# A fourth of twelve products for GpSimd in the second stage, with B brought by transfers

## The chip, the cores and the metric

The kernel runs on one core of one Trainium2 chip. The metric is the device time of one execution in microseconds (us), the median of several runs. All data are float32. A core has five engines with a queue of their own each: TensorE (PE in the profile, its weight loads PEld), VectorE (DVE), ScalarE (ACT), GpSimd (POOL), and SyncE (SP), which here issues nearly all transfers.

## The reference

Three stages follow one another on a batch of four images of 192 channels and 64 x 64 pixels: two Mamba layers read forwards (first stage), one Mamba layer with a depthwise convolution and an MLP (second stage), and a window network (third stage). The change is in the second stage's Mamba layer. Cut to what matters, with `L` = 4096 positions, 384 channels `d` and 16 states `n`:

```python
xz = xf @ in_w.T;  xm, z = split(xz)
xm = silu(conv1d(xm) + conv_b)                 # 3 taps
dt, B, C = split(xm @ x_w.T)                   # 12 + 16 + 16 rows
delta = softplus(dt @ dt_w.T + dt_b)
for t in range(L):                             # per channel d and state n
    h[d, n] = exp(delta[t, d] * A[d, n]) * h[d, n] + delta[t, d] * xm[t, d] * B[t, n]
    y[t, d] = sum_n h[d, n] * C[t, n]
y = (y + xm * D) * silu(z)
out = y @ out_w.T
```

## The kernel before

**Tiles.** Positions are cut into tiles of `T` = 512, so the second stage has 4 x 8 = 32 units (image, tile). The 384 x 16 states of a unit lie in 12 blocks; a block k is a tile of 128 partitions (16 channels x 8 states) by four column groups j of 512 positions. `unit["order"]` says in which order a unit takes its blocks; q counts the places 0 to 11 in it. Blocks 2p and 2p+1 form pair p: they have the same channels and differ in the half of the states, so they share the operands of their pair (`dtE`, delta repeated for the states; `dtxE`, delta times xm repeated), while `B` and `C` belong to one of the two halves of the states ("parity" k % 2).

**A step.** `Scans.run` goes through 32 x 48 steps, step i being column group j = i % 4 of the block at place q. `Scans.step` issues for it:

- `decay` (L923) for step i + 2: ScalarE makes dA = exp(dtE * A) in one of three PSUM buffers;
- `step` (L929): VectorE's scan of 512 positions over dA and h;
- at j = 3, `read` (L945): GpSimd multiplies the block's h by C, 128 x 2048; `keep` (L940) saves the states; `sum` (L955) lets TensorE add the states of a channel with four small matmuls, some steps later; and after every fourth block `skip` (L979, VectorE) and `gate` (L985, GpSimd) finish 128 channels;
- `product` (L916): h = dtxE * B for a whole block, 128 x 2048. For the places in `shared`, which are (3, 7, 11) here, GpSimd makes it, into `h_apart`, out of `Bs`, a copy of B that a transfer has spread over the partitions (`bring_B`). For the other nine VectorE makes it at the end of the block before, into `h`, out of `B`, which TensorE spreads with one matmul into a PSUM bank (`spread`, L886) out of `dbl`. In this stage h_apart has 1 buffer, h has 3.

**Transfers.** `load` (L879) brings the `dtE` of a pair at an even place and the `dtxE` at an odd one, each with four transfers of 256 KB (16 rows, repeated 8 times), two to three places ahead; both have 2 buffers. Their sources r_dt and r_dtx are DRAM rows, written by `front` once per unit. SyncE's queue takes all of them in program order, and a transfer that has to wait holds back those behind it.

**Work beside the scans.** Everything else of the stage (layer norms, projections, taps, the next unit's `front`, the output projection `back`, the convolution and the MLP) is cut into pieces. `Behind.tick` issues pieces after every step from five lanes, as far as a budget of TensorE and ScalarE time allows. The evictions of PSUM banks are put off by some steps (`later`), and the tables `AHEAD` (keys `l_...` for the evictions, `w_...` for waits between pieces) and the `wait=` numbers of the pieces set by how many. An activation with a table of its own (Silu, Softplus, Gelu) is a `burst`: it may go only where the next block's product is VectorE's (`edge`), and costs a table load before and after it. The order on each engine is thus fixed when the program is built.

**Fronts.** During unit n, `front` of unit n + 1 runs: projection, taps, Silu, `dbl`, the three `dt` evictions (L781), Softplus (L788), delta times xm on GpSimd (L789), the two stores to r_dt and r_dtx (L794), then the three z projections (L745, evicted at L754) and their Silu (L806).

Of the kernel before, what the change touches and what calls it, by code (L numbers as in the profile page):

```python
# [30 lines left out]
KX = 68  # L31
# [219 lines left out]
class Timeline:  # L251
# [131 lines left out]
AHEAD = {  # L383
    "a_back0": 0,
    "a_cv00": 2,
# [10 lines left out]
    "b_z": 2,  # L396
    "l_dt": -1,
    "l_dw": 1,
    "l_hid": 1,
    "l_mean1": 2,  # L400
    "l_o": 0,
    "l_out": 1,
    "l_rb2": 0,
    "l_tap": 0,
    "l_var1": 2,
    "l_var2": 0,
    "l_x": 1,
    "l_z": -1,
    "w_h1": 0,
    "w_h2": 4,  # L410
    "w_h3": 1,
    "w_in1": 0,
    "w_sq1": 2,
}

# [258 lines left out]
class Mamba:  # L674
# [3 lines left out]
    def __init__(  # L678
# [8 lines left out]
        self.nc, self.name, self.taps, self.ex, self.scan = nc, name, taps, ex, scan  # L687
        self.order = (1, 0, 2, 3, 4, 5, 7, 6, 9, 8, 10, 11) if summed else range(NQ)
        self.z_b = None
# [43 lines left out]
    def front(self, xn, first, u):  # L733
# [31 lines left out]
        for d in range(ND):  # L765
            nc.tensor.matmul(ps, self.x_w[:, d, :], xc[:, d, :], start=(d == 0), stop=(d == ND - 1))
        dbl = u["dbl"] = self.work.tile([KX, T], F32, name="dbl", bufs=2 if self.summed else 1)
        h = behind.later(lambda ps=ps: nc.scalar.copy(dbl, ps), name="x")
        halves = []
        for d in range(ND):  # L770
            yield Piece(0.85, bank=True, after=[h], wait=(1 if d else 3) if self.summed else (0 if d else 2))
            if d == 0:
                bc = u["bc"] = self.dram.tile([2 * NS, T], F32, name="r_bc", bufs=3)
                nc.sync.dma_start(bc, dbl[RK : RK + 2 * NS, :])
                dt = self.work.tile([128, ND, T + 4], F32, name="dt", bufs=1)[:, :, 3 : 3 + T]
                dtx = raw[:, :, K - 1 :]
            ps = behind.bank([128, T], "ps_dt")
            nc.tensor.matmul(ps, self.dt_w[:, bass.ts(d, 128)], dbl, start=True, stop=True)
            halves.append(
                behind.later(  # L780
                    lambda d=d, ps=ps: nc.scalar.activation(  # L781
                        dt[:, d, :], ps, AF.Identity, bias=self.dt_b[:, d : d + 1]
                    ),
                    name="dt",
                )
            )
# [10 lines left out]
        u["rows"] = rows  # L797
        z = u["z"] = self.work.tile([128, ND, T + 4], F32, name="z", bufs=2)[:, :, 1 : 1 + T]
        made = []
        for d in range(ND):  # L800
            if d:
                yield Piece(1.7, bank=True, wait=0)
            made.append(project(ND + d, z[:, d, :]))

        def silu():
            nc.scalar.activation(z, z, AF.Silu)  # L806
            u["silu"] = True
            yield Piece()
# [37 lines left out]
    def sum_taps(self, raw, projected, u):  # L846
# [3 lines left out]
        for d in range(ND):  # L850
# [6 lines left out]
            for j, o in enumerate((raw[:, d, 2:], one[:, d, 1:], xc[:, d, :])):  # L857

                def tap(o=o, ps=ps, d=d, j=j):
                    nc.scalar.activation(  # L860
                        o, ps, AF.Identity, scale=self.conv_w[:, d, j : j + 1], bias=self.tap_b[:, d, j : j + 1]
                    )

                h = behind.later(tap, bank=(j == 2), more=j, name="tap")
            halves.append(h)
        yield Piece(after=halves, wait=2)
        nc.gpsimd.tensor_copy(self.halo[:, :, :2], raw[:, :, T:])
# [6 lines left out]
    def load(self, u, pair, i):  # L874

        t = u["rows", pair, i] = self.work.tile([128, 4, T], F32, name=("dtE", "dtxE")[i], bufs=2)
        for j in range(4):
            row = 128 * (pair // 2) + 32 * j + 16 * (pair % 2)
            self.nc.sync.dma_start(  # L879
                t[:, j, :], u["rows"][i][row : row + 16, :].unsqueeze(1).broadcast_to([16, 8, T])  # L880
            )

    def spread(self, u, o, last):

        B = u["B", o] = self.psum_a.tile([128, T], F32, name="B" if self.summed else f"B{o}", bufs=1)
        self.nc.tensor.matmul(B, self.ex.spread[:, o, :], u["dbl"], start=True, stop=True)  # L886
        u["spread"][0] = last
# [14 lines left out]

    def bring_B(self, u, o):
        v = self.work.tile([128, 1 + T], F32, name="Bs", bufs=1)[:, 1:]
        rows = u["bc"][8 * o : 8 * o + 8, :]
        self.nc.sync.dma_start(v, rows.unsqueeze(0).broadcast_to([16, 8, T]))
        u["Bs", o] = v

    def product(self, u, k):
        apart = k in u["apart"]  # L910
        if apart:
            h = self.work.tile([128, 4, T + 4], F32, name="h_apart", bufs=1 if self.summed else 3)
        else:
# [7 lines left out]
    def decay(self, u, k, j):  # L921
        dA = u["dA", k, j] = self.psum_a.tile([128, T], F32, name="dA", bufs=3)
        self.nc.scalar.activation(  # L923
            dA, u["rows", k // 2, 0][:, j, :], AF.Exp, scale=self.A[:, k, j : j + 1]
        )
# [48 lines left out]
    def skip(self, u, c):  # L974
        y = u["xc"][:, c, :]
        if not self.summed:
            self.nc.vector.tensor_tensor(y, u["ys"], u["z"][:, c, :], ALU.mult)
            return
        self.nc.vector.scalar_tensor_tensor(y, y, self.D[:, c : c + 1], u["ys"], ALU.mult, ALU.add)  # L979

    def gate(self, u, c):
        if not self.summed:
            return
        y = u["xc"][:, c, :]
        self.nc.gpsimd.tensor_tensor(y, y, u["z"][:, c, :], ALU.mult)  # L985


class Scans:
# [6 lines left out]
    def __init__(self, nc, units, behind):  # L995
        self.nc, self.units, self.behind = nc, units, behind
        self.due = {}
        for n, unit in enumerate(units):
            unit[1]["y_read"], unit[1]["gated"] = [False], [False]
            xcs = unit[0].xcs  # L1000
            unit[1]["xc_free"] = [units[n - xcs][1]["y_read"]] if n >= xcs else []
            unit[1]["z_free"] = [units[n - 2][1]["gated"]] if n > 1 else []
            unit[1]["spread"] = [False]
            odd = int(n % 2 and unit[0].summed)
            unit[1]["order"] = [k ^ odd for k in unit[0].order]
            unit[1]["apart"] = [unit[1]["order"][q] for q in unit[0].shared]
            dbls = 2 if unit[0].summed else 1
            unit[1]["dbl_free"] = [units[n - dbls][1]["spread"]] if n >= dbls else []

# [8 lines left out]
    def run(self):  # L1018
# [3 lines left out]
        for o in range(2):  # L1022
            if o == (u["order"][0] % 2 if m.summed else 1):
                m.spread(u, o, not m.summed)
            self.behind.add(0, m.spread_C(u, o), Piece())
        if m.summed:
            m.bring_B(u, u["apart"][0] % 2)
        for i in range(2):
            m.load(u, 0, i)
        m.load(u, 1, 1)  # L1030
        self.behind.force(lambda: m.summed or ("Bs", 0) in u)
        m.product(u, u["order"][0])
        for i in range(self.AHEAD):
            m.decay(u, u["order"][0], i)
# [12 lines left out]
    def step(self, i, n):  # L1047
# [8 lines left out]
        if j == 0 and to < n:  # L1056
            m2, u2, k2, _ = self.tile(to)
            self.behind.force(lambda: "rows" in u2)
            m2.load(u2, k2 // 2, q % 2)
        if i + self.AHEAD < n:  # L1060
# [3 lines left out]
        if m.summed:  # L1064
            if j == 0 and k not in u["apart"]:
                self.spread(i, n, m, u, k)
        elif j == 0 and q == NQ - 1 and i + 8 < n:
# [3 lines left out]
        if j == 2 and i + 6 < n:  # L1071
            m2, u2, k2, _ = self.tile(i + 6)
            if k2 in u2["apart"]:
# [5 lines left out]
                if m2.summed and i3 < n:  # L1079
                    _, u3, k3, _ = self.tile(i3)  # L1080
                    self.at(i + 6, lambda: m2.bring_B(u3, k3 % 2))
        if j == 3:
# [6 lines left out]
            if i + 1 < n:  # L1089
                m2, u2, k2, _ = self.tile(i + 1)  # L1090
                if k2 not in u2["apart"]:
                    m2.product(u2, k2)
            added, skipped, gated = (4, 6, 8) if m.summed else (8, 12, 12)
            if q % 4 == 0 and not m.summed or q + 2 in m.shared and m.summed:
                added += 1 if m.summed else 2
            self.at(i + added, lambda: self.sum(m, u, q))
            if q % 4 == 3:
                c = q // 4
                self.at(i + skipped, lambda: self.skip(m, u, c))
                self.at(i + gated, lambda: m.gate(u, c))  # L1100
                if c == ND - 1:
                    self.at(i + gated, lambda: self.gated(u, after))

    def gated(self, u, after):
# [6 lines left out]

    def spread(self, i, n, m, u, k):
        i += 4
        while i < n and i // 4 % NQ in m.shared:
            i += 4
        if i >= n:
            return
        m2, u2, k2, _ = self.tile(i)
        if u2 is u and k2 % 2 == k % 2:
            return  # L1120
        rest = [k3 for k3 in u2["order"][i // 4 % NQ :] if k3 not in u2["apart"]]
        m2.spread(u2, k2 % 2, all(k3 % 2 == k2 % 2 for k3 in rest))
        self.behind.budget -= 0.85

# [202 lines left out]
def mamba_block(tc, x, p96, p96_ap, p128, p128_ap, m_in, ex_aps, out, sums, following):  # L1327
# [4 lines left out]
    with ExitStack() as ctx:  # L1332
# [18 lines left out]
        behind.order = (4, 1, 2, 3, 0)  # L1351
        behind.bl = 0.2
        ln = NormT(nc, const, work, behind)
        ex = Expand(nc, fixed, *ex_aps)
        mamba = Mamba(
            nc, "m", 3, m_in, const, work, fixed, scan, psum_y, psum_a, dram, ln.ident, ex, behind, (3, 7, 11), True
        )
# [95 lines left out]
        def tail(b, t):  # L1453
# [33 lines left out]
            for k in range(2):  # L1487
# [3 lines left out]
                )  # L1491
            yield Piece(1.7, bank=True, wait=5, after=[taken[0]])
            xn = work.tile([CP, 2, T], F32, name="xn2", tag="xn2", bufs=1)
            yield from ln.run(x2, xn, 2)
            units[b * NT + t]["past"][0] = True
            taken[0] = [False]
            behind.add(3, end(b, t, x2, xn, taken[0]), Piece(1.7, bank=True, wait=6))

# [33 lines left out]
        def after(n):  # L1532
# [4 lines left out]
            for t2 in ([t - 1] if t else []) + ([t] if t == NT - 1 else []):  # L1537
                ended = [units[b * NT + t2 - 2]["ended"]] if b * NT + t2 > 1 else []
                behind.add(2, tail(b, t2), Piece(2.6, bank=True, after=first + ended, wait=8))

# [847 lines left out]
```

## Time and profile before

| | |
|---|---|
| median of 3 runs | 9311.5 us (9307.59 to 9312.82) |
| the profiled execution's own time | 9300.5 us |
| its span, first to last instruction | 9298.7 us |
| first scan of the second stage to the end of its last | 4836.2 to 7638 us |
| one unit of the second stage, between 5550 and 6943 us | 87.1 us |
| TensorE's granted clock in that stretch | 0.99 |
| instructions of the whole program: DVE, POOL, ACT, PE | 7419, 3104, 10008, 30312 |
| blocks whose product VectorE, GpSimd makes (whole program) | 672, 480 |

How to read it: the page lists groups of instructions by line, engine, operation and operands (out<-in), with their count, busy time and mean duration, and then the idle time of the engine just ahead of them with what ended it. "DVE L916 h<-dtxE,B" is VectorE's product and "POOL L916 h_apart<-dtxE,Bs" is GpSimd's. The view by stretches gives the busy time of each engine in a window; the view of waits says which engine waited at which line for which; the timeline lists instructions with their starts. One float32 matmul of the program shows as two MATMUL records. The profiled execution lies 11.0 us under the median.

### The profile page before, as it was taken

The numbers are of one execution on the slowest core, as the hardware profiler recorded it, in microseconds if no ns is written. First come the engines' busy times: TensorE is split into PE (matmuls) and PEld (weight loads), VectorE is DVE, ScalarE is ACT, GpSimd is POOL, SyncE is SP. The second block draws the span as 40 slices with busy tenths as digits, with TensorE's granted clock in tenths as the row PEclk, the third lists the DMA queues.
The fourth block names the chain that finished last, engine by engine and source line by source line (L and its number), as shares of the span: only waits on it lengthen the run. The fifth ranks groups of instructions, "written<-read, shape, count | busy, mean of one in ns | idle before, by whom it ended". The sixth has DMA issues, their size and how long they took to land. (4 is left out here: it accounts for less than half of the span.)

```text
span 9298.7 us, 96768 instructions
## 1 busy us (share of the span) xinstructions
PE 7726.7 (83%) x30312; PEld 3365.2 (36%) x30312; DVE 8341.9 (90%) x7419; ACT 6520.0 (70%) x10008; POOL 7213.3 (78%) x3104
## 2 busy tenths in 40 slices
PE   5777777777777777777757999999999996899998
PEld 2322323223232232322222333333333333666766
DVE  7999999999999999999959999999999985766742
ACT  5777777777777777777746777878878863454543
POOL 6999999999999999999958888888888871111100
PEclk8888888888888888888867999999999998999999
DMA  7888888888888888888846676676676653223210
GB/s 191 213 210 209 217 213 214 210 209 216 214 213 211 209 214 214 214 212 209 215 126 182 174 193 189 184 193 189 183 194 188 184 151 79 51 64 77 52 42 22
DMA packets 1025037, 1614.02 MB, mean 174 GB/s; under 512 B 251476, under 2 KB 284584, under 8 KB 1024008
## 3 DMA queue, kind: packets, MB, share of 16 engines
q1 hardware_dynamic: 1023520, 1604.52, 66.1%
q8 instruction: 239, 3.92, 0.2%
q10 hardware_dynamic: 1000, 3.30, 0.1%
q14 instruction: 278, 2.28, 0.1%
HBM read 1388.05 MB, written 219.41 MB: 173 GB/s over the span
## 5 line engine op out<-in xcount | busy, mean ns | idle before, releaser
L923 ACT ACTIVATE dA<-dtE,m_A 128x512 f32<-128x512 f32 x4608 | 3125.6, 687 | 1355.7 <-DVE h L929 1048.2
L929 DVE TENSOR_TENSOR_SCAN h<-dA,m_state,h 128x512 f32<-128x512 f32 x2688 | 3254.6, 1266 | 91.7 <-ACT dA L923 56.0
L945 POOL TENSOR_TENSOR h<-h,C 128x2048 f32<-128x2048 f32 x672 | 2565.2, 3817 | 337.7 <-DVE h L929 246.1
L929 DVE TENSOR_TENSOR_SCAN h_apart<-dA,m_state,h_apart 128x512 f32<-128x512 f32 x1920 | 2301.1, 1260 | 49.2 <-POOL h_apart L916 47.0
L916 POOL TENSOR_TENSOR h_apart<-dtxE,Bs 128x2048 f32<-128x2048 f32 x480 | 1834.9, 3823 | 78.3 <-DMA Bs<-r_bc 32.8
L945 POOL TENSOR_TENSOR h_apart<-h_apart,C 128x2048 f32<-128x2048 f32 x480 | 1833.3, 3819 | 32.9 <-DVE h_apart L929 31.5
L916 DVE TENSOR_TENSOR h<-dtxE,B 128x2048 f32<-128x2048 f32 x672 | 1519.8, 2262 | 47.5 <-DMA dtxE<-r_dtx 47.2
L955 PE MATMUL y<-h_apart,gather 128*32 128x512 f32 x3840 | 651.0, 756 | 664.2 <-POOL h_apart L945 393.9
L1781 POOL TENSOR_TENSOR d<-d,rs 128x512 f32<-128x512 f32 x64 | 85.0, 1328 | 1250.2 <-DVE rs L1776 1250.2
L745 PE MATMUL ps_in<-xT,m_in_w 96*128 96x512 f32 x1536 | 875.2, 722 | 27.7 <-ACT z L755 27.7
L955 PE MATMUL y<-h,gather 128*32 128x512 f32 x5376 | 812.3, 679 | 70.1 <-POOL h L945 66.5
L832 PE MATMUL ps_conv<-raw,m_conv 128*128 128x512 f32 x1536 | 694.5, 601 | 54.2 <-ACT raw L755 35.8
L745 PEld LDWEIGHTS ps_in<-xT,m_in_w 96*128 96x128 f32 x1536 | 341.5, 235 | 653.5 <-issue 435.5
L1465 PE MATMUL ps_dw<-strip,dw 96*96 96x512 f32 x1152 | 529.1, 605 | 0.0
L886 PE MATMUL B<-dbl,spread 68*128 68x512 f32 x384 | 263.3, 773 | 303.2 <-DVE h L916 283.6
L955 PEld LDWEIGHTS y<-h_apart,gather 128*32 128x32 f32 x3840 | 86.0, 118 | 1054.6 <-POOL h_apart L945 547.5
L832 PEld LDWEIGHTS ps_conv<-raw,m_conv 128*128 128x128 f32 x1536 | 282.3, 190 | 464.9 <-issue 417.6
L923 ACT ACT_TABLE_LOAD x343 | 440.1, 1283 | 13.6 <-DMA dtE<-r_dt 7.6
L1991 PE MATMUL unit<-xn,sed 64*128 64x256 f32 (+3 forms) x2944 | 405.5, 383 | 8.8 <-DVE d L1753 5.1
L630 PE MATMUL ps_h<-xn,t 96*128 96x512 f32 x768 | 368.3, 619 | 29.7 <-ACT xc L860 22.1
L650 PE MATMUL ps_o<-hid,t 128*96 128x512 f32 x768 | 362.9, 611 | 33.5 <-ACT hid L643 33.5
L745 PE MATMUL ps_in<-xn,m_in_w 96*128 96x512 f32 x768 | 362.5, 623 | 28.3 <-DVE xn L604 28.2
(208 smaller groups left out, 11238.3 us busy)
## 6 DMA issues: line engine op xcount, KB each, us to landing
dtE<-r_dt SPq DMA_DIRECT2D x2304, 256.0 KB, 5.8
dtxE<-r_dtx SPq DMA_DIRECT2D x2304, 256.0 KB, 4.3
r_dt<-dt SPq DMA_DIRECT2D x96, 768.0 KB, 4.6
r_dtx<-raw SPq DMA_DIRECT2D x96, 768.0 KB, 6.3
C<-r_bc SPq DMA_DIRECT2D x192, 256.0 KB, 4.9
Bs<-r_bc SPq DMA_DIRECT2D x160, 256.0 KB, 5.4
x<-x SPq DMA_DIRECT2D x64, 384.0 KB, 3.7
img<-x SPq DMA_DIRECT2D x28, 512.0 KB, 7.7
```

The source lines that it names most:

```text
L630: nc.tensor.matmul(ps, self.w1[:, k, bass.ts(m, 128)], x[:, k, :], start=(k == 0), stop=(k == 1))
L650: nc.tensor.matmul(ps, self.w2[:, m, bass.ts(k, CP)], h[:, m, :], start=(m == 0), stop=(m == NH - 1),)
L745: nc.tensor.matmul(ps, self.in_w[:, k, bass.ts(e, 128)], xn[:, k, :], start=(k == 0), stop=(k == 1))
L832: nc.tensor.matmul(ps, self.conv[:, d, j, :], raw[:, d, j : j + T], start=(j == 0), stop=(j == K - 1))
L886: self.nc.tensor.matmul(B, self.ex.spread[:, o, :], u["dbl"], start=True, stop=True)
L916: engine.tensor_tensor(h[:, :, 1 : 1 + T], u["rows", k // 2, 1], u[B, k % 2].unsqueeze(1).broadcast_to([128, 4, T]), ALU.mult)
L923: self.nc.scalar.activation(dA, u["rows", k // 2, 0][:, j, :], AF.Exp, scale=self.A[:, k, j : j + 1])
L929: self.nc.vector.tensor_tensor_scan(h[:, j, 1 : 1 + T], u.pop(("dA", k, j)), h[:, j, 1 : 1 + T], self.state[:, k, j : j + 1], ALU.mult, AL ...
L945: nc.gpsimd.tensor_tensor(h[:, :, :T], h[:, :, 1 : 1 + T], u["C", k % 2].unsqueeze(1).broadcast_to([128, 4, T]), ALU.mult)
L955: self.nc.tensor.matmul(u["ys"][32 * j : 32 * j + 32, :], self.ex.gather[:, i // 2, :], h[:, j, :T], start=(i == 0), stop=(i == 3 and self ...
L1465: nc.tensor.matmul(ps, dw[:, k, j, :], s[:, k, dy : dy + rows, dx : dx + HW], start=(j == 0), stop=(j == 8),)
L1991: nc.tensor.matmul(out, sed[p, int(h is not None), i ^ position(k, s), cols], xn[b, g].t[p, c, :], start=start, stop=stop,)
```

## The change

GpSimd makes the products at places 3, 7, 9 and 11, into two buffers of h_apart. TensorE spreads no B in this stage; for the other eight products a transfer brings B into a new tile `Bd`, and ScalarE copies it to the PSUM bank `B` where the half of the states changes, four times a unit (`fill` sets the places). `dtE` becomes a ring of five single parts (one column group each), whose four transfers are issued at four successive steps; `z` becomes a ring of five single parts, so Silu on z is three activations, and the third z projection waits until the unit before has gated its first 128 channels (`z_gate`). `dbl` has one buffer. `Bs` is brought for the next GpSimd block 2 steps after the product ahead of it is issued, where it was 6, and not where the half stays the same. `sum` is issued one step earlier. The delays of this stage (`l_...`, `w_...`, `wait=`, `bl`) have other values. The first stage's instructions are the same.

```diff
-    "l_dt": -1,
+    "l_dt": 0,
...
-    "l_o": 0,
+    "l_mean2": 1,
+    "l_o": 2,
...
+    "w_rb1": 4,
+    "w_rb2": 8,
...
-        z = u["z"] = self.work.tile([128, ND, T + 4], F32, name="z", bufs=2)[:, :, 1 : 1 + T]
+        if self.summed:
+            z = u["z"] = []
...
-                yield Piece(1.7, bank=True, wait=0)
+                yield Piece(1.7, bank=True, after=u["z_gate"] if d == ND - 1 else (), wait=1 if self.summed else 0)
+            if self.summed:
+                z.append(self.work.tile([128, T + 1], F32, name="z", bufs=5)[:, 1:])
...
         def silu():
-            nc.scalar.activation(z, z, AF.Silu)
+            for v in z if self.summed else (z,):
+                nc.scalar.activation(v, v, AF.Silu)
...
-                h = behind.later(tap, bank=(j == 2), more=j, name="tap")
+                h = behind.later(tap, bank=(j == 2), more=0, name="tap")
...
+    def load_dt(self, u, pair, j):
+        t = u["dtE", pair, j] = self.work.tile([128, T], F32, name="dtE", bufs=5)
+        self.part(t, u, pair, 0, j)
...
+    def spread(self, u, o, last=False):
         B = u["B", o] = self.psum_a.tile([128, T], F32, name="B" if self.summed else f"B{o}", bufs=1)
+        if self.summed:
+            self.nc.scalar.copy(B, u["Bd", o])
+            return
         self.nc.tensor.matmul(B, self.ex.spread[:, o, :], u["dbl"], start=True, stop=True)
...
-            h = self.work.tile([128, 4, T + 4], F32, name="h_apart", bufs=1 if self.summed else 3)
+            h = self.work.tile([128, 4, T + 4], F32, name="h_apart", bufs=2 if self.summed else 3)
...
-            m2.load(u2, k2 // 2, q % 2)
+            if m2.summed and q % 2 == 0:
+                for j2 in range(4):
+                    self.at(i + 1 + j2, lambda m=m2, u=u2, p=k2 // 2, j=j2: m.load_dt(u, p, j))
+            else:
+                m2.load(u2, k2 // 2, q % 2)
...
-            if j == 0 and k not in u["apart"]:
-                self.spread(i, n, m, u, k)
+            if i in self.due_fills:
+                u2, o = self.due_fills[i]
+                m.spread(u2, o)
...
-                    self.at(i + 6, lambda: m2.bring_B(u3, k3 % 2))
+                    if u3 is not u2 or k3 % 2 != k2 % 2:
+                        self.at(i + 2, lambda: m2.bring_B(u3, k3 % 2))
...
-            added, skipped, gated = (4, 6, 8) if m.summed else (8, 12, 12)
+            added, skipped, gated = (3, 6, 8) if m.summed else (8, 12, 12)
...
+    def fill(self):
+        n = len(self.units) * NQ
+        self.due_fills, before, held = {}, 0, None
+        for at in range(n):
+            m, u, k, _ = self.tile(4 * at)
+            if k in u["apart"]:
+                continue
+            if held not in (None, (id(u), k % 2)):
+                i = 4 * before + 1
+                self.due_fills[i] = u, k % 2
+                self.at(max(i - 5, 0), lambda m=m, u=u, o=k % 2: m.bring_B(u, o, "Bd"))
+            before, held = at, (id(u), k % 2)
...
-        behind.bl = 0.2
+        behind.bl = 0.6
...
-            nc, "m", 3, m_in, const, work, fixed, scan, psum_y, psum_a, dram, ln.ident, ex, behind, (3, 7, 11), True
+            nc, "m", 3, m_in, const, work, fixed, scan, psum_y, psum_a, dram, ln.ident, ex, behind, tuple((3, 7, 9, 11)), True
```

## The prediction

> **What bounds the kernel now.** I read the stretches first, then the groups of one of them, the waits, and the timeline of one unit. From 5410 us on, the second stage repeats every 87.1 us (the product ahead of a unit's first scan starts at 5550.08 and, 16 units on, at 6943.44), so 16 units stand for the stage.
>
> ```profile
> core 0: us, PE busy (x) PEld busy (x) DVE busy (x) ACT busy (x) POOL busy (x), PEclk, DMA share, GB/s
> 5410.00:6802.00 1392.00, 1348.01 (x4670) 513.13 (x4669) 1372.24 (x1122) 1117.10 (x1455) 1206.46 (x705) 0.99 0.70 188
> ```
>
> VectorE is busy 1372 of 1392 us (98.6%), TensorE, whose ends are modelled, 97%, GpSimd 87%, ScalarE 80%. The groups of the same stretch say of what VectorE's time is made, and what one product costs on either engine:
>
> ```profile
> L929 DVE TENSOR_TENSOR_SCAN h<-dA,m_state,h 128x512 f32<-128x512 f32 x576 | 705.0, 1267 | 19.4 <-ACT dA L923 9.3
> L916 DVE TENSOR_TENSOR h<-dtxE,B 128x2048 f32<-128x2048 f32 x144 | 325.6, 2261 | 0.3 <-PE B L886 0.2
> L929 DVE TENSOR_TENSOR_SCAN h_apart<-dA,m_state,h_apart 128x512 f32<-128x512 f32 x192 | 231.1, 1258 | 0.0
> ...
> L945 POOL TENSOR_TENSOR h<-h,C 128x2048 f32<-128x2048 f32 x144 | 549.2, 3814 | 151.5 <-DVE h L929 116.7 <-PE rb L596 30.3 <-PE B L886 4.4
> L916 POOL TENSOR_TENSOR h_apart<-dtxE,Bs 128x2048 f32<-128x2048 f32 x48 | 183.2, 3816 | 0.0
> ```
>
> VectorE's idle time is some 20 us in 16 units, and GpSimd mostly waits for VectorE's scans: VectorE sets the pace. TensorE is next: only its in-order queue and the transfers could take over. The unit's end on SyncE and VectorE's product, from the timeline:
>
> ```profile
> 5696.57 0.39 SPq L794 DMA_DIRECT2D r_dt<-dt  x1
> 5697.01 3.21 SPq L879 DMA_DIRECT2D dtE<-r_dt  x4
> 5700.31 0.54 SPq L794 DMA_DIRECT2D r_dtx<-raw  x1
> 5701.06 0.33 SPq L1512 DMA_DIRECT2D x<-x  x1
> 5706.79 2.95 SPq L879 DMA_DIRECT2D dtxE<-r_dtx  x4
> ...
> 5675.03 2.26 DVE L916 TENSOR_TENSOR h<-dtxE,B 128x2048 f32<-128x2048 f32 x1
> 5677.39 2.46 DVE L929 TENSOR_TENSOR_SCAN h<-dA,m_state,h 128x512 f32<-128x512 f32 x2
> ```
>
> The reader is to see that dtxE waits at the head of SyncE's queue for r_dtx to land, and that a product takes 2.36 us from its start to the next scan's.
>
> **What the Trainium skill says.** "SBUF — State Buffer", Who interferes with whom: a VectorE instruction with at most one SBUF input doesn't contend with GpSimd, one with two does. The trace agrees: product and scan have one operand in PSUM (B, dA), and scans last 1252 to 1287 ns beside a GpSimd busy 87%. The changed B still lies in PSUM, so I keep 2.26 us. "TensorE: Matmul & The Clock Gate", Architectural detail: ScalarE, VectorE and GpSimd are strict FIFO, and TensorE pulls only weight loads ahead; so whatever is issued behind a waiting instruction waits too. "DMA: Bandwidth & Descriptors", Anatomy of one DMA: a transfer's semaphore wait happens on the issuing sequencer; the 6.5 us between r_dtx and dtxE above are that. "ScalarE: Activation LUTs", What ACT_TABLE_LOAD costs: 1283 ns and a drain of 1380. The trace has 1283 ns and the next activation right behind (5693.77, then 5695.06), so a load counts 1.28 us.
>
> **The change part by part**, per unit; durations are start to start in the timeline.
>
> 1. VectorE loses one product: -2.36 us, 32 times = **-75.5 us**. Counting a unit of VectorE after (48 scans of 1.18, 8 products of 2.36, or 2.18 ahead of anything but a scan, two layer norms at 2 x 1.12, skips 3 x 0.64, MLP and strip 2 x 0.66 and 2 x 0.58) gives 84.1 us without a wait; the same count for before gives 86.4, so 0.7 of its 87.1 is waiting.
> 2. GpSimd gains 3.77 us: its instructions sum to 79.1 us of some 85. Followed along its queue from the unit's first scan (t = 0), the products for places 3, 7, 9, 11 end at 12.9, 43, 61.6 and 73, and are wanted at 20.7, 49.4, 62.9 and 78: hidden, through the second buffer (place 9's product is made before place 7's h is read). Cover at place 9: 1.3 us.
> 3. TensorE loses four B matmuls (5729.49 to 5730.45: 0.96 us each), 3.8 us; its sum falls from 84.5 to 80.7. It was not setting the pace, so nothing by itself, but its queue no longer waits for VectorE's product ahead of each B.
> 4. ScalarE gains four copies (nearest row: COPY raw<-ps_in, 0.59 us) and 0.25 us for Silu in three parts (3 x 0.58 for 1.49): +2.6 on 70 us, beside VectorE. A copy waits for nothing on VectorE that the decay ahead of it hasn't waited for. At places 0 and 4 it stands before a burst; there Silu on xc ends with its loads at 34.3 and the next decay at 35.0, wanted at 35.8: hidden with 0.8 us.
> 5. New waits on TensorE's queue. Softplus's inputs: Gelu on `hid` ends at 42.0; `dbl` is copied behind that burst, at 45.7; then in program order dt, MLP output, dt, dt, MLP output, sum, MLP output x 4, sum, rb, MLP output x 2: 14.6 us of matmuls (0.9 each, sums 1.0) to 60.4, and the first z projection ends at 62.2. Its eviction stands before the decay for place 9, which so ends at 63.6, where VectorE arrives at 62.9: **+0.75**; the sum of place 7 behind the z projections ends at 66.8, and `skip` waits +0.2. Behind that eviction the decays of place 9 and the other two z evictions queue, and VectorE waits for the decays. Before, the z evictions (from 5701.96) ended without a wait of VectorE. Bounds 0 (if TensorE runs 1 us ahead of my count) and 2.4 (if `dbl` comes 1.5 later).
> 6. SyncE gets four more transfers (0.6 us of issue each) and dtE one by one. The `Bs` for place 11 now stands before the store to r_dtx and waits for place 9's product: r_dtx goes at 62.2 rather than at 57.8, and behind it queue three dtE parts, the next unit's dtxE, Bd and the last dtE part. Then r_dtx lands (4.0, as r_dt does ahead of its four dtE; 6.4 as r_dtx did behind them), dtxE x4 (2.95), Bd (0.6), and only then the fourth dtE part of places 10 and 11 (landing median 5.2, 3.3 to 8.1). With 4.0 it is there at 75, its decay at 76, and VectorE wants it at 76.8: hidden, 0.6 to 0.8 us to spare. With 6.4 it costs +1.3, with 8.1 on top +4.2. I take 4.0, since nothing large is queued ahead of r_dtx any more: +0.
> 7. Edits costed at nothing, with their cover: each dtE part waits for the decay that frees its buffer, and is wanted five scans later, 5 x 1.18 = 5.9 us or more against a landing of 5.2; ScalarE's decay runs up to three dA buffers ahead of its scan, which covers the rest. `z_gate` is set by a gate that ends near 47.9, ahead of the z projections. The one `dbl` is read last by dt matmuls a unit earlier. With `sum` a step earlier TensorE waits 0.8 us for GpSimd's h of place 3, and 0.8 at place 4 for `skip`; both lie ahead of the wait for Gelu, so nothing moves.
> 8. The retuned delays: +0.4 for small misfits, which leaves about half of the 0.7 of waiting that there is now. Bounds -0.7 (a gain, if the new order fits better than the old) and +1.5.
>
> A unit after: 84.1 + 0.95 + 0.4 = 85.45; 87.1 - 85.45 = 1.65; x 32 = **-53 us**. At the edges the list of instructions leaves 6 more matmuls behind the last scan (6 x 0.9 = 5.4 us), and the first B comes by a transfer (5.1, Bs's median): **+10**, bounds -10 and +25 as the third stage is ordered around that drain. Sum -43. The profiled execution, 9300.5 (span 9298.7, 1.8 around it), becomes 9257; the median stood 11.0 above it, so **9268 us**.
>
> **Rivals.** (a) All hidden: the new waits are 0 and VectorE's product comes off whole, 9311.5 - 75.5 = 9236. For it: idle of 20 us in 16 units now. Against: part 5. (b) TensorE's queue takes over: the z chain is later by 1.5 us more (its clock was 0.80 to 0.92 until 5323, and the chain is matmuls), so a unit keeps 87: 9311 to 9320. (c) The other side: the fourth dtE part behind r_dtx decides. Its cover of 0.7 us is gone when r_dtx takes 4.8; it eats the 1.65 us of gain when the chain is 2.4 us longer (6.4 to land), and at 6.4 with a dtE landing 1.8 above its median a unit takes 88.8 or +1.75: 9311.5 + 56 = 9368. For it: six 256 KB transfers then stand in a row. Against: the DMA share is 0.70. (d) It does other than it says: the list of instructions has 640 and 512 products for 672 and 480, 128 copies for 128 B matmuls, and no other count moves; as good as excluded.
>
> **How the numbers follow.** Forecast 0.47, (a) 0.24, both faster; (b) 0.15, of which 0.09 within 0.2% and 0.06 above; (c) 0.12, slower; (d) or anything unforeseen 0.02, slower. A measurement of this kernel tells about 0.2% (19 us) from no change. Faster 0.71, same 0.09, slower 0.20. The range runs from (a) with 8 us more at the edge, 9228, to 9330, which takes in (b) and the milder third of (c). The forecast's own range is 9248 to 9290.
>
> **What would show it.** Right: VectorE's product group counts 640 and stays at 2.26 us, GpSimd is busy about 93% of a steady stretch, a unit takes 85 to 86 us, and VectorE's waits name dA at the place after z's eviction. Wrong: h_apart scans waiting for GpSimd's product (part 2), dA waiting for dtE (part 6, rival c), products longer than 2.3 us, or a unit of 87.

## The result and the profile after

The changed kernel takes 9442.5 us (median of 4 runs, 9433.2 to 9454.2) against 9312.2 before: ratio 1.0142, 95% interval 1.0129 to 1.0154. It is **130 us slower**; 43 us less was forecast. The profiled execution took 9433.2 us, its span 9431.4.

Cut at three instructions that every kernel here has (the starts of VectorE's first scan of the stage, of its last, and of its last addition `x<-ps_o`), the profiled spans divide as follows, in us:

| | to the first scan | scans | last scan to last addition (the drain) | rest (third stage) | span |
|---|---|---|---|---|---|
| before | 4836.2 | 2800.9 | 235.8 | 1425.8 | 9298.7 |
| after | 4837.9 | 2891.3 | 266.8 | 1435.4 | 9431.4 |
| difference | +1.7 | +90.4 | +31.0 | +9.6 | +132.7 |

First the same stretch as before, 16 units between two resets of the scan's state. They now take 1449 us, 90.6 each for 87.1.

```profile
5565.00:7014.00 1449.00, 1353.75 (x4544) 500.60 (x4543) 1349.86 (x1106) 1137.97 (x1550) 1265.32 (x722) 0.95 0.73 192
```

The third busy time is VectorE's: 1350 for 1372 us before, so it does lose work, but it is busy 93% of the time instead of 98.6%. The groups of this stretch say where the idle time is:

```profile
L950 DVE TENSOR_TENSOR_SCAN h<-dA,m_state,h 128x512 f32<-128x512 f32 x512 | 628.3, 1269 | 64.2 <-ACT dA L944 55.4 <-DVE h L937 0.5
L944 ACT ACTIVATE dA<-dtE,m_A 128x512 f32<-128x512 f32 x767 | 507.2, 685 | 182.9 <-DMA dtE<-r_dt 149.0 <-DVE h L950 29.6 <-DVE h_apart L950 0.2
...
L950 DVE TENSOR_TENSOR_SCAN h_apart<-dA,m_state,h_apart 128x512 f32<-128x512 f32 x256 | 314.4, 1270 | 34.9 <-ACT dA L944 34.9
L937 DVE TENSOR_TENSOR h<-dtxE,B 128x2048 f32<-128x2048 f32 x128 | 289.7, 2263 | 0.0
...
L937 POOL TENSOR_TENSOR h_apart<-dtxE,Bs 128x2048 f32<-128x2048 f32 x64 | 244.0, 3812 | 0.0
```

VectorE's product is as long as before (2263 ns) and waits for nothing: B, made by a transfer and ScalarE's copy, is there in time. The scans wait for decays, and ScalarE's decays wait for `dtE` transfers (149 us of idle time in 16 units). The waits between 4900 and 7600 us (line waited at, releaser; total us, times, longest) say the same. Before, where h_apart's scans waited for a decay once (0.8 us) and no line names `dtE` for ScalarE:

```profile
ACT dA L923 <- DVE h L929: 244.4, 254, 3.8
...
DVE h L929 <- ACT dA L923: 27.2, 44, 2.0
```

and after:

```profile
ACT dA L944 <- DMA dtE<-r_dt: 285.3, 95, 9.2
...
DVE h L950 <- ACT dA L944: 107.7, 140, 4.6
...
DVE h_apart L950 <- ACT dA L944: 73.4, 84, 7.4
...
DVE h_apart L950 <- POOL h_apart L937: 0.2, 1, 0.2
```

What was late is in the timeline of one place, SyncE's queue first (start, length; a group that is "x3" long stands still inside it):

```profile
6032.82 8.93 SPq L895 DMA_DIRECT2D dtE<-r_dt  x3
6041.85 2.47 SPq L895 DMA_DIRECT2D dtxE<-r_dtx  x4
6044.36 0.60 SPq L927 DMA_DIRECT2D Bd<-r_bc  x1
6045.05 13.85 SPq L895 DMA_DIRECT2D dtE<-r_dt  x4
```

and, in a narrower stretch, the third of those first parts:

```profile
6041.24 0.52 SPq L895 DMA_DIRECT2D dtE<-r_dt  x1
```

and ScalarE's at the same time:

```profile
6040.52 0.69 ACT L944 ACTIVATE dA<-dtE,m_A 128x512 f32<-128x512 f32 x1
...
6042.45 0.70 ACT L944 ACTIVATE dA<-dtE,m_A 128x512 f32<-128x512 f32 x1
...
6051.71 0.69 ACT L944 ACTIVATE dA<-dtE,m_A 128x512 f32<-128x512 f32 x1 [3.78 <-DMA dtE<-r_dt]
6052.34 0.57 ACT L905 COPY B<-Bd 128x512 f32<-128x512 f32 x1
```

The third dtE part of the place goes out at 6041.24, right when the decay that started at 6040.52 has freed its buffer. The fourth part's buffer is freed by the next decay in the list, at 6043.15. But four dtxE and one Bd stand ahead of it: it goes out at 6045.05, 1.9 us after it could, with five transfers of 256 KB right in front of it on the wires, and lands 6.6 us later (the median of dtE in this stretch of the stage is 5.0). ScalarE is free at 6047.9 and stands 3.8 us for it. In this unit it happens at three places, 4, 10 and the next 0, each time with the fourth part. Counted by the number of the decay over the whole stretch, 4900 to 7600 us, ScalarE's 285 us stand at place 0 (121 us), 4 (76), 10 (56), 6 and 8 (32 together), and all but 0.9 us of them at the fourth part.

### The profile page after: what moved, and what is told of

Same layout as the page of the kernel before. It is cut to its first block, busy times and chain, and to the rows that moved or that the text cites. A ratio compares the mean times of both kernels' runs of the same rounds, so it can differ in the third digit from the quotient of the medians.

```text
span 9431.4 us, 97376 instructions
## 1 busy us (share of the span) xinstructions
PE 7722.0 (82%) x30056; PEld 3342.4 (35%) x30056; DVE 8294.6 (88%) x7387; ACT 6559.9 (70%) x10198; POOL 7328.8 (78%) x3136
## 5 line engine op out<-in xcount | busy, mean ns | idle before, releaser
L950 DVE TENSOR_TENSOR_SCAN h<-dA,m_state,h 128x512 f32<-128x512 f32 x2560 | 3102.0, 1267 | 169.3 <-ACT dA L944 137.5
L966 POOL TENSOR_TENSOR h<-h,C 128x2048 f32<-128x2048 f32 x640 | 2440.8, 3814 | 237.3 <-DVE h L950 201.4
L950 DVE TENSOR_TENSOR_SCAN h_apart<-dA,m_state,h_apart 128x512 f32<-128x512 f32 x2048 | 2467.7, 1263 | 123.7 <-ACT dA L944 74.5
L937 POOL TENSOR_TENSOR h_apart<-dtxE,Bs 128x2048 f32<-128x2048 f32 x512 | 1955.1, 3819 | 63.4 <-DMA Bs<-r_bc 32.5
L966 POOL TENSOR_TENSOR h_apart<-h_apart,C 128x2048 f32<-128x2048 f32 x512 | 1953.3, 3815 | 6.0 <-DVE h_apart L950 4.8
L937 DVE TENSOR_TENSOR h<-dtxE,B 128x2048 f32<-128x2048 f32 x640 | 1448.9, 2264 | 46.7 <-DMA dtxE<-r_dtx 46.7
L976 PE MATMUL y<-h_apart,gather 128*32 128x512 f32 x4096 | 689.5, 751 | 680.9 <-POOL h_apart L966 412.9
L1511 PE MATMUL ps_dw<-strip,dw 96*96 96x512 f32 x1152 | 560.6, 635 | 0.0
L656 PE MATMUL ps_o<-hid,t 128*96 128x512 f32 x768 | 408.3, 670 | 7.9 <-ACT hid L649 6.7
L751 PE MATMUL ps_in<-xn,m_in_w 96*128 96x512 f32 x768 | 368.7, 626 | 42.3 <-DVE xn L610 34.5
L795 POOL TENSOR_TENSOR raw<-dt,xc 128x1536 f32<-128x1536 f32 x96 | 279.1, 2907 | 113.0 <-ACT dt L794 110.0
```

What stands on the lines that cost most here:

```text
L656: nc.tensor.matmul(ps, self.w2[:, m, bass.ts(k, CP)], h[:, m, :], start=(m == 0), stop=(m == NH - 1),)
L751: nc.tensor.matmul(ps, self.in_w[:, k, bass.ts(e, 128)], xn[:, k, :], start=(k == 0), stop=(k == 1))
L937: engine.tensor_tensor(h[:, :, 1 : 1 + T], u["rows", k // 2, 1], u[B, k % 2].unsqueeze(1).broadcast_to([128, 4, T]), ALU.mult)
L950: self.nc.vector.tensor_tensor_scan(h[:, j, 1 : 1 + T], u.pop(("dA", k, j)), h[:, j, 1 : 1 + T], self.state[:, k, j : j + 1], ALU.mult, AL ...
L966: nc.gpsimd.tensor_tensor(h[:, :, :T], h[:, :, 1 : 1 + T], u["C", k % 2].unsqueeze(1).broadcast_to([128, 4, T]), ALU.mult)
L976: self.nc.tensor.matmul(u["ys"][32 * j : 32 * j + 32, :], self.ex.gather[:, i // 2, :], h[:, j, :T], start=(i == 0), stop=(i == 3 and self ...
```

## The experiments

"The better order" below means that the fourth dtE part goes out ahead of the dtxE transfers of its place. All ratios are to the kernel before on the same chip, with 95% intervals.

### 1. The order in SyncE's queue

Edit to the changed kernel, in `step` and `fill` (dtxE and Bd after the fourth part):

```diff
+            elif m2.summed:
+                self.at(i, lambda m=m2, u=u2, p=k2 // 2: m.load(u, p, 1))
...
-                self.at(max(i - 5, 0), lambda m=m, u=u, o=k % 2: m.bring_B(u, o, "Bd"))
+                bring = lambda m=m, u=u, o=k % 2: m.bring_B(u, o, "Bd")
+                if i < 6:
+                    self.at(0, bring)
+                else:
+                    self.at(i - 6, lambda at=i - 5, bring=bring: self.at(at, bring))
```

> The changed kernel with another order on SyncE's queue: at an odd place the fourth dtE part goes first, then Bd, and the four dtxE transfers last. Queue theory: the fourth dtE part lands late because it stands behind four dtxE and Bd, which in turn stand behind the third part's wait for a decay; ScalarE then waits at dA and VectorE for dA. Moved ahead it lands some 3 us earlier, a unit goes from 90.6 to 86 to 88 us, ScalarE's wait for dtE from 295 to under 100 us, and the time to 9280 to 9350 us. Load theory (ScalarE's copies and Silu parts make the decays late) and delay theory (the retuned delays do): within 20 us of 9442.

Measured: 9296.2 us, ratio 0.9985 (0.9978 to 0.9992), as the queue theory had it. One exchange in a queue takes back 146 us. Which of the two things in front did the harm, a run with the first two lines of the edit alone was to tell; Bd stays ahead of the fourth part:

> The changed kernel with one difference: the four dtxE transfers of a place are issued after the fourth dtE part. Bd stays where it was, just ahead of that part. It tells which of the two things ahead of the fourth part did the harm. Theory A1 (the four dtxE, 2.5 us of issue, with the third part's wait ahead of them): nearly all of the better order's gain of 146 us is there, 9290 to 9320. Rival A2 (Bd, since the waits fell on the places that have one): half of the gain or less, 9370 to 9440.

Measured: 9292.3 us, 0.9980 (0.9973 to 0.9987), as good; below, this run is "the dtxE order". So it is the four dtxE; without them, Bd's 0.6 us in front of a part is harmless. SyncE's timeline of this run, and its waits between 4900 and 7600 us:

```profile
6021.24 0.59 SPq L927 DMA_DIRECT2D Bd<-r_bc  x1
6022.33 0.51 SPq L895 DMA_DIRECT2D dtE<-r_dt  x1
6022.94 2.47 SPq L895 DMA_DIRECT2D dtxE<-r_dtx  x4
```

```profile
DVE h_apart L950 <- ACT dA L944: 52.1, 73, 7.4
...
DVE h L950 <- ACT dA L944: 10.5, 16, 1.1
...
ACT dA L944 <- DMA dtE<-r_dt: 2.9, 1, 2.9
```

ScalarE's wait for dtE goes from 285 to 3 us. A unit takes 85.9 us (5540.9 to 6915.7 for 16).

### 2. The ring by itself, put into the kernel before

The kernel before with nothing of the change but its ring of five dtE parts, each sent at a step of its own:

```diff
+        t = u["dtE", pair, j] = self.work.tile([128, T], F32, name="dtE", bufs=5)
...
+            if m2.summed and q % 2 == 0:
+                for j2 in range(4):
+                    self.at(i + 1 + j2, lambda m=m2, u=u2, p=k2 // 2, j=j2: m.load_dt(u, p, j))
```

> The kernel before with one part of the change alone: dtE in a ring of five single parts, issued one per step. Queue theory: the third part waits for a decay at the head of SyncE's queue, four dtxE behind it, the fourth part after those; ScalarE waits for dtE, a unit goes from 87.1 to 88.5 to 90.5 us, the time to 9360 to 9420 us. Load and delay theory: no change, 9312 us within 20.

Measured: 9394.8 us, 1.0093 (1.0076 to 1.0110), within the queue theory's range. The wait is there without Bd, without a fourth product and with the old delays:

```profile
ACT dA L928 <- DMA dtE<-r_dt: 204.4, 104, 8.3
...
DVE h L934 <- ACT dA L928: 73.9, 88, 4.4
...
DVE h_apart L934 <- ACT dA L928: 8.9, 18, 0.7
```

Two runs then cured it in two ways: more buffers with the order as it was (`bufs=8`, the room that the kernel before had), or the better order with five buffers.

> The kernel before, its dtE loaded in single parts, one at each of four steps, in a ring of EIGHT single buffers (the room of the two buffers of four that it had). The fourth part still stands in SyncE's queue behind the four dtxE transfers, as in the ring of five. Theory A (the queue behind a wait for a freed part: with eight parts the buffer that a transfer wants was freed four scans earlier than with five, so nothing in the queue stands still): 9305 to 9325, and ScalarE's waits for dtE back to some 10 us of the 200 of the ring of five. Rival B (it is the issue one by one, or the fourth part's place behind dtxE by itself, not the freeing): as with the ring of five, 9380 to 9410.

> The kernel before with the ring of FIVE single dtE parts, and one difference to that run: the four dtxE transfers of a place come after the fourth dtE part instead of ahead of it. Theory A (the harm is that the fourth part stands behind the dtxE transfers, which stand behind a third part that waits for its buffer): 9305 to 9340, ScalarE's waits for dtE under 60 us. Rival C (a ring of five is too short for any order: the part lands after its decay is due): 9370 to 9400.

Measured: 9311.8 us, 1.0001 (0.9992 to 1.0010), with eight; 9312.1 us, 1.0002 (0.9993 to 1.0010), with five in the better order: theory A both times. ScalarE's waits for dtE are 12.4 us in 13 waits with eight, and there is no such line with five. The two runs differ in SyncE's waits for dtE's buffers, between 4900 and 7600 us. With eight buffers:

```profile
SPq L886 <- ACT dA L928: 51.6, 106, 2.7
```

and with five in the better order:

```profile
SPq L886 <- ACT dA L928: 1311.8, 405, 12.8
```

(1339.7 us in 340 waits in the ring of five that lost 85 us.) All of SyncE's waits in that stretch together are nearly the same in the three runs: 1621 us with eight buffers, where the queue stands for other things (so "nothing in the queue stands still" did not come true), 1651 with five in the better order and 1652 in the run that lost 85 us. So how long the queue stands still does not tell the two kinds apart. Standing costs nothing as long as no transfer behind the waiting one is wanted sooner than it can land from there.

### 3. What the fourth product and TensorE's relief are worth

The better order (both edits of experiment 1) with places (3, 7, 11) in `shared`, so that VectorE makes nine products:

> The changed kernel in the better order (fourth dtE part, Bd, dtxE) with GpSimd making three of the twelve products (places 3, 7, 11) instead of four; VectorE makes nine. It tells what the fourth product is worth. Theory A (VectorE is the bound once the queue is in order; a product costs it 2.26 us and GpSimd's handing over no more than some tenths): one product in each of 32 units more, +65 to +80, that is 9360 to 9380. Rival D (something else, TensorE or the latency of the decays, bounds the unit at 86 us): +0 to +30, 9296 to 9326.

Measured: 9355.4 us, 1.0045 (1.0029 to 1.0062), 59 us more than with four and just under theory A's range; the scans' stretch is 2813.6 us against 2754.6. That is 1.84 us a unit, for 2.36 that VectorE's product takes. The delays here are those that came with four products. They may account for part of that difference, and for why three products are slower here than in the kernel before.

TensorE's matmul for VectorE's B, back in place of Bd and the copies:

```diff
-        if self.summed:
-            self.nc.scalar.copy(B, u["Bd", o])
-            return
         self.nc.tensor.matmul(B, self.ex.spread[:, o, :], u["dbl"], start=True, stop=True)
...
-        dbl = u["dbl"] = self.work.tile([KX, T], F32, name="dbl", bufs=1)
+        dbl = u["dbl"] = self.work.tile([KX, T], F32, name="dbl", bufs=2 if self.summed else 1)
```

It was first tried in the changed kernel's own queue order, with a charge of 0.85 us for the matmul in the planner's budget:

> The changed kernel with B spread by TensorE's matmul again (two dbl buffers), so without the Bd transfers and the ScalarE copies; everything else as changed. Queue theory: SyncE's queue has 0.6 us less ahead of the fourth dtE part at four places, and ScalarE 2.3 us less per unit, so a unit loses 1 us or so of its waiting: 9390 to 9430 us. Load theory: the waits for dA go with the copies, 75 us or more are won: 9370 us or less. Delay theory: within 20 us of 9442.

Measured: 10032.7 us, 1.0777 (1.0761 to 1.0794), far outside of all three. Then again without the charge, with the dtxE order and with the drain's old delays (experiment 4):

> The changed kernel with dtxE after the fourth dtE part and the drain's delays of before, and VectorE's B made by TensorE's matmul as before (two dbl buffers, no Bd, no copies on ScalarE), this time without the charge of 0.85 us for it in the planner. It tells why making B by matmul cost 590 us, and what the transfers of B are worth. Theory M1 (the charge and the bad queue order made that loss): some 4 us a unit more TensorE work beside a VectorE that bounds, 9265 to 9340. Rival M2 (B's matmul stands in TensorE's queue behind work that waits, and VectorE's product waits for it, or the tail falls behind, whatever the planner counts): over 9500.

Measured: 9370.2 us, 1.0066 (1.0050 to 1.0083), above M1's range and far below M2's. Against 9264.4 for the same kernel with transfers of B (experiment 4), the transfers and copies are worth 106 us in this structure, with its delays. The waits between 4900 and 7600 us show the direct part of it:

```profile
DVE h L968 <- PE B L938: 69.4, 54, 4.7
DVE h_apart L981 <- ACT dA L975: 65.9, 90, 7.5
```

VectorE's product waits for TensorE's B, which it hardly did in the kernel before. The charge, the order and the drain's delays were changed together between the two runs, so how the other 660 us divide was not separated. The order and the drain are worth 146 and 32 us elsewhere in this study; the rest, including the charge, is open.

### 4. The delays and the drain

The changed kernel with all delays (`AHEAD`, `wait=`, `bl`, `sum`) of the kernel before:

> The changed kernel with all delays of the second stage as they were (eviction delays, waits of pieces, burst limit, sum at 4 steps). Queue theory: the scans keep some 90 us a unit, and only the drain after the last scan, which took 266 us instead of 236, goes back: 9400 to 9425 us. Delay theory: the scans go back to 87 us or less and the time to 9320 us or less. Load theory: as the queue theory.

Measured: 9774.1 us, 1.0496 (1.0480 to 1.0512). Every expectation missed: the retuned delays don't cost some 20 us, they are worth 332 in the changed kernel. So the old delays don't fit the new structure; which of them does it was not tried.

The better order, and ahead of the drain's call alone, when the last scan is out:

```diff
+        AHEAD.clear()
+        AHEAD.update(OLD_AHEAD)      # the table of the kernel before
+        behind.bl = 0.2
         behind.drain(beside)
```

> The changed kernel in the better order; after the last scan, while what is left of the stage's tail is drained beside the third stage's start, the delays in the table and the threshold of the Gelu are those of the kernel before. It tells whether the drain's 263 us (235 in the kernel before) come from the retuned delays. If so: 25 to 30 us less than the better order alone, 9266 to 9272. If the drain is longer because the tail is further back when the scans end, or for another reason: within 5 us of 9296.

Measured: 9264.4 us, 0.9951 (0.9936 to 0.9966), 32 us less than the better order alone. From the last scan to the last addition it takes 242.4 us instead of 264.6. VectorE's wait for the MLP's output in that stretch, after (the better order alone has 35.4 us, the longest 25.0 too):

```profile
DVE x L1547 <- PE ps_o L656: 35.3, 3, 25.0
```

and with the drain's old delays:

```profile
DVE x L1587 <- PE ps_o L690: 17.6, 3, 7.6
```

(before: 20.6 us in 4 waits, the longest 6.2). As the code has it, a delay counted in steps is filled by scans as long as there are scans; in the drain there are none, and the MLP's chain just stands. The table and `bl` were changed together, so their shares are open.

A last run brought Bs two steps later on top of that (`self.at(i + 4, ...)` for `i + 2`):

> The changed kernel in the better order and with the drain's delays of before (9264 us), and Bs brought two steps later, four steps after the product that frees its buffer was given out instead of two, when GpSimd has ended it or is about to, so that SyncE stands before it less (343 us in 92 waits without this). Theory A (nothing on ScalarE or VectorE waits for what stands behind Bs any more): the wait at Bs falls to under 150 us and the time stays, 9258 to 9270. Rival E (the r_dt and r_dtx transfers behind it still come late for the next unit): 10 to 30 us less, 9235 to 9255.

Measured: 9261.6 us, 0.9951 (0.9936 to 0.9966), in theory A's range. SyncE's wait for GpSimd's product falls from 343 to 194 us (not to under 150), its waits for dtE's buffers rise from 927 to 1044, and all its waits together stay at 1556 and 1555: the standing moved, and the time is the same. These last two kernels beat both of the given ones, by 45 and 48 us against before.

The stretches of the main runs together, in us:

| | scans | drain | rest |
|---|---|---|---|
| before | 2800.9 | 235.8 | 1425.8 |
| before, ring of five | 2879.4 | 236.0 | 1429.3 |
| before, ring of eight | 2800.7 | 235.9 | 1435.7 |
| after | 2891.3 | 266.8 | 1435.4 |
| after, dtxE order | 2754.6 | 264.5 | 1434.8 |
| after, better order, old delays in the drain | 2751.1 | 242.4 | 1432.7 |

## Why the prediction was wrong, point by point

**Part 1 (VectorE loses a product) held.** 640 products of 2264 ns; a unit's work without waits was counted at 84.1 us, and in the dtxE order the unit takes 85.9 against the 85.45 of the sum. The scans' stretch there is 46 us shorter than before; -53 was said. So the sum of parts 1 to 8 was right to half a microsecond a unit for a kernel in which the queue doesn't bite. VectorE's waits for decays there are 2.0 us a unit: 0.8 at place 9, where part 5 has them, and 0.8 at place 3, where the taps' evictions run between the decays and no part named a wait.

**Part 2 held:** GpSimd was busy 87% (1265 of 1449 us) since the unit grew, and 92% in the dtxE order (93 was said); VectorE waited for its product once, 0.2 us. **Part 4 held:** no product waited for a copy. **Part 3** took TensorE's relief as worth nothing by itself. The run with the matmul put back says up to 106 us, with delays that were made for a TensorE without it; in the kernel before, TensorE's B made VectorE wait 0.2 us in 16 units. The cost of an operation that wasn't the bound depended on the plan around it.

**Part 5 (z's chain) held.** In the run with the dtxE order, ScalarE waits 2.62 us for the first z projection, the decays behind it are late, and the scan of h_apart at 6035.06 waits 0.57 us; +0.75 was said. (Its list of matmuls gives 12.8 us as written. The trace has two MLP outputs at each of its first two mentions, which gives the 14.6 that it used; 6017.29 to 6031.76 were measured.)

**The step that failed is in part 7,** the sentence on the ring's cover: "each dtE part waits for the decay that frees its buffer, and is wanted five scans later, 5 x 1.18 = 5.9 us or more against a landing of 5.2". It counts the landing from the moment the buffer is free. For the fourth part it has to be counted from the moment that SyncE gets to it. The third part leaves when its own buffer is freed; then come four dtxE (2.5 us of issue), Bd and the gaps (3.8 us from the third part's issue to the fourth's), while the fourth's buffer is free 1.9 us after the third's. So 1.9 us must be added, and the landing behind five large transfers was 6.6 and not 5.2: 8.5 against 5.9. At the place shown ScalarE came for the part 4.8 us after its buffer was free and stood 3.8; its lead over the scans covered most of that, and VectorE stood 0.86:

```profile
6052.44 1.28 DVE L950 TENSOR_TENSOR_SCAN h<-dA,m_state,h 128x512 f32<-128x512 f32 x1 [0.86 <-ACT dA L944]
```

The prediction had the rule at hand, from the Trainium skill ("DMA: Bandwidth & Descriptors", Anatomy of one DMA: a transfer's wait stands on the issuing sequencer), and used it for r_dtx alone; the ring put into the kernel before agrees with it, 85 us for what stood behind. Measured over the stretch, ScalarE waited 3.0 us each (285.3 / 95), and VectorE, by its waits for decays in the two queue orders, lost 4.1 us a unit more (181.1 in 2700 / 90.6 units against 62.6 in 2700 / 85.9). 32 of these are 131 us, against the 137 by which the scans' stretch differs between the two orders.

Only half of the 4.1 us stands at the scans of the late parts themselves: 61.8 us in 29.8 units at places 0, 4 and 10, 2.1 a unit. The rest stands at later scans, mostly at places 5, 7, 8 and 9, and goes with the exchange too; by what path is open. At place 7 the trace shows a part of it: in 14 units VectorE stands there, 17.3 us in all, and in 13 of them TensorE's granted clock had been at 0.50 for 6.8 us or more some 45 us into the unit (6065.7 to 6072.5 in the unit shown, where ScalarE then stands 2.4 us for a `ps_dt` of TensorE). From the seventh unit on, those without this wait had the 0.50 for 3.4 us there.

**Part 6** looked for this very thing behind r_dtx at the unit's end, once a unit, and took it as hidden, with r_dtx landing in 4.0 us and 0.6 to 0.8 to spare. (Its +1.3 for a landing of 6.4 is 1.6 by its own times, 76 + 2.4 - 76.8.) r_dtx landed in 4.9, and rival (c) had the cover gone at 4.8. So it was, at the place of which part 6 speaks, 10:

```profile
6086.76 0.58 SPq L800 DMA_DIRECT2D r_dtx<-raw  x1
...
6091.84 2.44 SPq L895 DMA_DIRECT2D dtxE<-r_dtx  x4
...
6095.02 0.54 SPq L895 DMA_DIRECT2D dtE<-r_dt  x1
```

ScalarE then stands 1.2 us at 6100.59. In the stretch SyncE stands for r_dtx in each of 30 units (41.0 us) and ScalarE for the fourth part of place 10 in 26 (55.9 us), so the +0 was too low here. But most of ScalarE's wait, 197 of 285 us, is at places 0 and 4, where no r_dtx stands ahead. There the third part's wait for its buffer holds the dtxE back, a wait that the kernel before had not (its SyncE stood at the group of four, with eight buffers). Rival (c) thus had the right end of the chain, the fourth part on SyncE's queue, the right sign, and the right trigger for one place of three; the other two it didn't see, and its 9368 was too low.

**Part 8** put the delays at +0.4 a unit. The unit in the dtxE order agrees (85.9 for 85.45), but what it called small misfits was the tuning of a structure: 332 us when undone.

**The edges** were to be +10: the first B's transfer and 5.4 us of matmuls left over. They were +42.3. The start took +1.7. The drain took +31.0, of which 22 go with the delays kept in it; the matmuls left over were counted, the waits of the chain between them were not. The third stage's +9.6 isn't the change's: with the ring of eight in the kernel before it is 1435.7 too, without a time lost.

Sum of the errors: scans 143.4 (90.4 for -53), edges 32.3, and -1.7 since the median lies 9.3 and not 11.0 above the profiled execution: 9268 + 174.0 = 9442.

## What to carry to other kernels

When a group of transfers is split into single ones that each wait for a buffer, read the issuing queue line by line: ask of every transfer who stands in front of it and what that one waits for, and count its landing from its issue, not from the moment its buffer is free. A ring may be cut in size at no cost if what is wanted first also goes out first; a long standing queue is no fault by itself (SyncE stood 1574 of 2700 us before, 1646 after and 1559 in the dtxE order). And delays counted in steps need another value where the steps that fill them end.

## What the hardware showed that was not expected

The same 256 KB transfer lands sooner or later by what was sent just ahead of it. With dtxE first, dtE has a median of 5.0 us between 4900 and 7600 us and dtxE 4.8; with the fourth dtE part first, 4.0 and 5.4. TensorE's granted clock was 0.95 in the 16 units of after and 0.99 in 16 units of the dtxE order and of before; why was not tried, and whether the lower clock is cause or effect of the waits is open. And the third stage, which no edit here touches, took 1425.8 to 1435.7 us in the kernels of the last table of the experiments, one execution each.
